# A four-layer graph kernel on one core: layer normalisation's last step on GpSimd, the loops of the graph selected later, and new orders of the jobs

## The chip, the cores and the metric

The kernel runs on one core of a Trainium2 chip. A core has a matrix engine (TensorE, called PE in the profile, with the loading of its weights as PEld), a vector engine (VectorE, DVE), a scalar engine (ScalarE, ACT), GpSimd (POOL) and SyncE (SP), which here only issues DMAs. Each engine works through a queue of its own in order. The metric is the device time of one execution in microseconds (us); lower is better.

## The reference

Input are x, 32 batches of 512 nodes with 64 features, and one graph adj of 512 x 512, symmetric in its pattern, sparse, with a full diagonal. Four layers follow one another, each as "normalise, clip at zero, graph operation, add":

```python
    # --- layer 0 (adj_preln) ---
    h = jnp.maximum(_layernorm(x, axis=-1), 0.0)
    x = x + _L0_gnn_ref(h, adj, ...)
    # --- layer 1 (adj_preln) ---
    h = jnp.maximum(_layernorm(x, axis=-1), 0.0)
    x = x + _L1_gnn_ref(h, 0, L1_gnn_net_params, adj)
    # --- layer 2 (adj_preln) ---
    h = jnp.maximum(_layernorm(x, axis=-1), 0.0)
    x = x + _L2_gnn_ref(h, adj, ...)
    # --- layer 3 (adj_preln) ---
    h = jnp.maximum(_layernorm(x, axis=-1), 0.0)
    x = x + _L3_gnn_ref(h, adj, ...)
```

Layer 0 is three steps of `W2 relu(W1 [v, adj v] + b1) + b2`; before them node 0 of v is set to a given row (`causal_vars.at[:, 0].set(intervention_value)`). Layer 1 is two steps of `relu((adj z) W)`. Layer 2 is attention with eight heads and an output head: scores `h h^T * graph`, zeros of the graph masked, softmax, a weighted sum. Layer 3 is attention with scores made of two vectors, on the graph with its diagonal set to 1 (`adj.at[diag].set(1.0)`). The normalisation is `(x - mean) / sqrt(var + 1e-5)` over the 64 features.

## The kernel before

**Tiling.** Batches go in 16 pairs; a pair's tile has 128 partitions (nodes) and 4 x 2 x 64 columns (node blocks, batches, features). On PE most matmuls use parts of the array: 64 x 64 quarters for scores, 32 x 64 strips for weighted sums, 128 rows for products with the graph. All is fp32, except the mask that is added to the scores.

**Jobs and their order.** The program consists of small named jobs, and three written lists say in which order they are emitted: HEAD (start, with all of pair 0 and much of pair 1), ROUND (once per pair in the middle; `name:lag` means the job of the pair that many rounds back), and TAIL (the last pairs). The lists set the order of each engine's queue; no scheduler changes it. The jobs that are spoken of below, for a pair p:

- `F0` to `F32`: the front, a generator cut at its yields: the layer norm of x (`F0` to `F2`), layer 0 (`F3` to `F20`; `F20` makes x1, L579), the norm of x1 (`F21` to `F23`), layer 1 (`F24` to `F29`; L485 is the product with the graph, L599 makes x2) and the norm of x2 (`F30` to `F32`). `zT` and `zE` turn the result for layer 2 (L473, L478) and copy its halves to the other partitions by DMA (ZZ). `ZQ..` spread z for the weighted sums by DMA.
- Layer 2 has eight units a, b, c, d (first batch) and g, h, i, j (second batch), and f for the output head. For a unit: `s` scores (PE, L641 and L644), `r` row maxima times the graph (DVE, L650), `m` their negation (POOL, L663), `x` exponentials (ACT, L670), `nA`/`nB` the reciprocal (DVE, L680) and the normalising (POOL, L682), `t` block transposes (DVE, L688). For two units: `k`/`Y` the products before the scores (L1139, L1150), `vA` to `vD` the weighted sum (PE, L697), `us`, `w`, `y`, `o`, `c` what follows it, `c` being the sum over heads (cat, L770 and L772).
- Layer 3 is unit e; `oA` to `oC` its norm, `vAE` to `vDE` the weighted sum of f and of the previous pair's e (L925). The last pair does these by batch (O0, O1, L0, L1).
- One-time jobs, in HEAD: `weights`, `joined`, `biases`, `bjoined`, `grams`, `vectors` (weights), `graph0` to `graph3` (the graph turned, L344), `masks` (L367), `factor0` to `factor3` (in place on A2, a copy of the graph, DVE, L371) and `loops0` to `loops3`, which set the diagonal of another copy, A3, to 1: four selects on POOL each (L376). A3 is the last of the three copies of the graph that SP loads (L290, L310, L317) and is used by layer 3 alone.

**The layer norm.** `ln_relu` runs 65 times: four per pair (three in the front, one in `oA` to `oC`), the last pair's fourth in two halves. It has three stages: mean on DVE (L419, L421), centring and squares on POOL (L423, L425); the variance on DVE (L428, L430) and the power -1/2 on POOL (r, L432); last z = max(xc, 0) * r on DVE (L435). In the first of a pair L541 then writes node 0's row into z on DVE and L542 adds a bias to x on POOL.

**The order in HEAD.** loops1, loops0 and loops3 stand between `0.F9` and `0.F12`, in POOL's queue after pair 1's first stage (`1.F0`) and ahead of its second (`1.F1`). In DVE's queue `1.F2` (z of pair 1) and then factor3 stand ahead of `0.F20` (x1 of pair 0).

Of the kernel before, what the change touches and what calls it, by code (L numbers as in the profile page):

```python
# [21 lines left out]
def gnn_stack_kernel(  # L22
# [40 lines left out]
        0.weights 0.F0 0.joined 0.F1 0.F2 0.F3 0.F4 0.biases 0.F5 0.F6 0.graph2 0.graph3 0.graph1 0.graph0 1.F0 0.F7  # L63
        0.F8 0.bjoined 0.F9 0.loops1 0.loops0 0.F10 0.F11 0.masks 0.loops3 0.F12 1.F1 0.factor1 0.F13 0.F14
        0.factor2 0.F15 0.F16 0.F17 1.F2 0.factor3 0.F18 0.grams 0.F19 0.F20 1.F3 2.F0 0.F21 0.F22 0.F23 0.F24 0.F25
        0.F26 1.F4 0.F27 1.F5 0.factor0 0.F28 0.F29 1.F6 0.F30 1.F7 0.F31 1.F8 0.vectors 0.F32 2.F1 0.zT 0.zE 0.k0
        0.Y0 1.F9 0.s0a 1.F10 0.s1a 0.r1a 0.ZQ11 0.r0a 0.r2a 0.m0a 0.x0a 0.s3a 0.r3a 0.s2a 0.m1a 0.r7a 0.r6a 0.r4a
        0.ZQ13 0.x1a 0.s1b 0.m3a 0.r5a 0.s0b 0.k1 0.x3a 0.m2a 0.x2a 0.nAa 0.r3b 0.r2b 0.r1b 0.r0b 0.m1b 0.Y1 0.s3b
        0.nBa 0.t0a 0.r6b 0.s2b 0.r4b 0.r7b 0.x1b 0.m0b 0.ZQ01 0.t1a 0.x0b 0.ZQ03 0.r5b 0.s0c 0.s1c 0.m2b 0.m3b
        0.t2a 1.F11 0.x2b 0.nAb 0.r1c 0.r2c 0.x3b 0.r0c 0.r3c 0.nBb 0.t3a 1.F12 0.t0b 0.m1c 0.t1b 0.m0c 0.x1c 0.s3c  # L70
        1.F13 0.ZQ02 1.F14 0.t3b 0.ZQ00 0.ZQ10 0.x0c 0.t2b 0.r7c 0.r6c 0.s2c 0.vA0 0.vB0 0.r4c 2.F2 0.r5c 0.m3c
        0.s0d 0.m2c 0.vC0 0.vD0 0.r1d 0.nAc 0.r0d 0.s1d 0.m0d 0.x3c 0.t0c 0.x2c 0.us0 0.s2d 0.t1c 0.w00 0.x0d 0.w10
        0.nBc 0.r3d 0.y00 0.r2d 0.t2c 0.m1d 0.t3c 0.ZQ12 0.r5d 0.s3d 0.r7d 0.k2 0.loops2 0.r6d 0.y10 0.o0 0.x1d
        0.r4d 0.m3d 0.Y2 0.x3d 0.m2d 0.nAd 0.c0 0.x2d 0.s1g 1.F15 1.F16 0.r2g 0.s0g 0.t0d 0.nBd 0.t1d 0.r3g 0.t2d
        1.F17 0.t3d 0.s3g 1.F18 0.r7g 0.vA1 0.r6g 0.vB1 1.F19 0.r0g 0.r1g 0.m1g 0.vC1 3.F0 1.F20 0.m3g 0.x1g 0.vD1
        0.m0g 0.s0h 0.s1h 0.r0h 0.r1h 0.us1 0.w01 0.s2g 0.x0g 0.r3h 0.r2h 0.x3g 0.s2h 0.y01 0.k3 0.nAg 0.m0h 0.r4g
        0.r5g 1.F21 0.r4h 0.r5h 0.Y3 0.m2g 0.t0g 0.x2g 0.s3h 0.w11 0.r6h 0.m2h 0.m1h 0.s2i 0.y11 0.nBg 0.x1h 0.x2h
        0.t1g 1.F22 0.r4i 0.s0i 0.t2g 1.F23 1.F24 0.r7h 0.m3h 0.r5i 0.x3h 0.x0h 3.F1 0.s1i 0.r0i 0.nBh 1.F25 0.r1i
        0.o1 0.r3i 0.t3g 0.r2i 0.nAh 1.F26 0.t2h 0.t3h 0.m0i 1.F27 0.t0h 0.t1h 0.s3i 1.F28 0.s1j 0.c1 1.F29 0.m1i
        1.F30 0.x1i 0.vA2 0.r6i 0.m2i 0.vB2 0.x2i 0.x0i 0.vC2 0.r7i 0.vD2 0.s2j 0.r2j 0.m3i 1.F31 0.x3i 0.nAi 0.r3j  # L80
        0.us2 1.F32 1.zT 0.m1j 2.F3 0.nBi 0.s0j 1.zE 0.r5j 0.r4j 2.F4 0.w12 0.t0i 0.x1j 2.F5 0.t2i 0.s3j 1.ZQ00 2.F6
        0.r1j 0.r7j 1.k0 0.y12 0.r0j 0.r6j 0.w02 0.m2j 0.m0j 1.Y0 0.x2j 1.s0a 1.s1a 2.F7 0.t1i 1.r1a 0.m3j 0.t3i
        0.x0j 0.x3j 0.y02 0.nAj 1.r3a 1.r0a 0.D0 1.r2a 2.F8 1.ZQ01 0.t0j 1.m1a 0.o2 1.k1 1.s3a 0.nBj 1.x1a 0.f0
        1.s2a 0.t1j 0.t2j 1.Y1 0.c2 1.m0a 0.t3j 0.vA3 0.vB3 1.ZQ02 1.r4a 1.x0a 1.r5a 1.nAa 0.vC3 0.vD3 1.m2a 1.r7a
        0.us3 1.t1a 1.x2a 3.F2 1.r6a 1.m3a 1.t0a 1.s1b 1.s0b 1.r2b 1.x3a 1.r3b 1.m1b 1.x1b 2.F9 1.ZQ10 1.r1b 1.ZQ12
        1.r0b 1.m0b 2.F10 1.x0b 1.s3b 1.ZQ11 1.s2b 1.nBa 1.r7b 1.r4b 1.r6b 1.m3b 0.w13 1.r5b 1.t2a 0.y13 0.w03 1.x3b
        1.m2b 1.s1c 1.nAb 1.t3a 1.x2b 1.r3c 1.t0b 1.s0c 1.nBb 1.r2c 0.y03 1.r0c 2.F11 2.F12 1.t1b 1.t2b 1.m1c 1.ZQ03
        1.r1c 0.o3 1.s3c 1.t3b 2.F13 1.s2c 1.m0c 0.c3 2.F14 1.r5c 1.x0c 1.vA0 0.D1 1.x1c 1.r6c 1.r4c 1.nAc 1.vB0
        0.f1 1.vC0 1.t0c 1.r7c 1.m2c 1.t1c 1.vD0 0.hQ0 1.x2c 1.s0d 1.us0 1.r1d 1.r0d 1.s1d 1.r3d 1.m3c 1.r2d 1.w00
        1.s2d 1.x3c 1.m0d 1.y00 0.hQ1 1.m1d 1.nBc 1.r4d 1.r5d 1.s3d 1.m2d 1.r6d 1.r7d 1.w10 1.m3d 1.t2c 1.x1d 1.x0d  # L90
        1.nAd 1.y10 1.x3d 1.x2d 0.s3f 1.t3c 1.t0d 0.s1f 1.k2 0.r3f 2.F15 0.hQ2 1.Y2 2.F16 1.nBd 0.r2f 1.o0 1.t1d
        1.t2d 2.F17 0.s0f 1.ZQ13 1.t3d 1.c0 2.F18 0.r7f 1.vA1 0.r1f 1.s0g 0.r6f 0.r0f 0.s2f 2.F19 1.vB1 0.m3f 1.r0g
        1.vC1 0.m0f 2.F20 0.r4f 1.r1g 1.m0g 0.r5f 0.x0f 0.m2f 4.F0 1.vD1 1.s1g 0.x3f 1.us1 0.m1f 1.s3g 2.F21 0.x2f
        1.r3g 1.r2g 1.w01 0.x1f 1.r6g 1.s0h 1.w11 1.m1g 1.r7g 0.nBf 1.r0h 1.s1h 1.x1g 1.r1h 1.s2g 1.y11 0.t2f 0.t3f
        0.nAf 1.x0g 2.F22 1.m0h 1.r5g 1.r2h 1.y01 1.o1 1.m3g 1.r4g 1.r3h 1.m2g 2.F23 0.hQ3 0.t0f 1.x3g 2.F24 1.nAg
        1.x2g 2.F25 0.t1f 1.c1 1.s2h 1.s3h 1.x0h 1.m1h 1.r4h 1.r5h 1.m2h 1.r7h 1.nBg 1.x2h 0.vAE 1.t0g 0.vBE 1.x1h
        0.vCE 0.vDE 0.eu 1.r6h 1.k3 1.t1g 0.et 1.nAh 1.t2g 1.Y3 1.m3h 1.t0h 1.s1i 0.er 1.s0i 1.t3g 1.r2i 2.F26 1.r1i
        1.x3h 1.r3i 1.nBh 2.F27 1.s3i 1.t1h 2.F28 1.r0i 1.t2h 1.t3h 2.F29 1.m1i 2.F30 1.s2i 1.r6i 1.m0i 1.x1i 1.vA2
        1.vB2 1.x0i 1.r7i 1.m3i 1.vC2 1.r4i 1.r5i 2.F31 1.vD2 1.x3i 0.oA 2.F32 1.m2i 1.nAi 1.s1j 1.us2 2.zT 0.oB
        1.r2j 2.zE 1.r3j 1.s0j 1.f0 1.r1j 1.r0j 1.x2i 1.w12 1.y12 1.s3j 3.F3 3.F4 1.m0j 1.s2j 2.ZQ01 2.k0 1.t0i  # L100
        1.r6j 1.w02 1.r7j 1.r5j 1.x0j 1.r4j 2.Y0 2.s0a 2.s1a 1.m3j 1.m1j 2.ZQ02 1.m2j 1.y02 3.F5 1.x1j 1.nBi 3.F6
        1.o2 1.t1i 1.x3j 2.r0a 1.t2i 1.x2j 1.nAj 2.r1a 3.F7 2.r3a 1.t0j 1.D0 1.c2 1.nBj 1.t3i 2.k1 2.r2a 2.m0a 1.t1j
        1.t3j 2.s2a 1.t2j 2.s3a 3.F8 2.m1a 2.Y1 2.r4a 2.x0a 2.r5a 1.vA3 2.r7a 2.x1a 1.vB3 2.nAa 1.vC3 2.m2a 4.F1
        2.t1a 2.x2a 1.vD3 2.t0a 2.r6a 2.s1b 2.s0b 2.m3a 1.us3 0.oC 2.r3b 2.r2b 2.x3a 2.r0b 1.w03 2.m1b 3.F9
    """
    ROUND = """
        r1b:0 s3b:0 y03:1 m0b:0 nBa:0 ZQ00:0 F10:-1 s2b:0 r7b:0 r6b:0 r4b:0 x1b:0 r5b:0 w13:1 ZQ11:0 hQ0:1 x0b:0
        y13:1 t2a:0 s0c:0 m2b:0 m3b:0 x3b:0 nAb:0 s1c:0 t3a:0 x2b:0 r1c:0 F11:-1 t0b:0 r0c:0 nBb:0 r3c:0 t1b:0 r2c:0
        F12:-1 t2b:0 ZQ03:0 o3:1 c3:1 s3c:0 F13:-1 m1c:0 t3b:0 oT:2 s2c:0 m0c:0 F14:-1 r4c:0 f1:1 x1c:0 oE:2 vA0:0
        r7c:0 x0c:0 vB0:0 r5c:0 vC0:0 vD0:0 r6c:0 m3c:0 D1:1 x3c:0 m2c:0 x2c:0 us0:0 nAc:0 t0c:0 nBc:0 t1c:0 s1d:0  # L110
        t2c:0 r2d:0 oN:2 s0d:0 w00:0 r3d:0 oV:2 r1d:0 s2d:0 r0d:0 s3d:0 m1d:0 r4d:0 x1d:0 m0d:0 w10:0 r5d:0 y00:0
        x0d:0 r7d:0 m2d:0 oD:2 oF:2 r6d:0 s1f:1 m3d:0 x2d:0 x3d:0 nAd:0 F15:-1 de:2 r3f:1 t3c:0 t0d:0 nBd:0 r2f:1
        y10:0 k2:0 t1d:0 t2d:0 F16:-1 t3d:0 o0:0 Y2:0 s6e:2 ZQ10:0 F17:-1 hQ1:1 c0:0 F18:-1 s0e:2 vA1:0 r0e:2 F19:-1
        s3e:2 s7e:2 r7e:2 s1e:2 vB1:0 r3e:2 s2e:2 r6e:2 lQ2:2 s0f:1 r2e:2 m3e:2 r1e:2 m1e:2 s5e:2 m0e:2 s4e:2 x0e:2
        m1f:1 F20:-1 r0f:1 x1e:2 hQ2:1 r5e:2 r1f:1 x3e:2 vC1:0 r4e:2 m2e:2 s3f:1 x2e:2 F21:-1 s2f:1 x1f:1 nAe:2
        vD1:0 m0f:1 us1:0 r7f:1 r6f:1 r4f:1 t0e:2 nBe:2 s0g:0 r5f:1 t1e:2 r1g:0 hQ3:1 m3f:1 s1g:0 x0f:1 w01:0 r2g:0
        r0g:0 w11:0 m2f:1 x3f:1 y01:0 nAf:1 x2f:1 m0g:0 r3g:0 t3e:2 t0f:1 y11:0 s3g:0 t2e:2 nBf:1 lQ1:2 x0g:0 lQ0:2
        s2g:0 r7g:0 r6g:0 F22:-1 m1g:0 F23:-1 o1:0 r4g:0 r5g:0 lQ3:2 t1f:1 m3g:0 s1h:0 m2g:0 t2f:1 c1:0 F24:-1 t3f:1
        x1g:0 F25:-1 ZQ12:0 s0h:0 x3g:0 nAg:0 r0h:0 r3h:0 r2h:0 x2g:0 vAE:1 r1h:0 m0h:0 m1h:0 vBE:1 vCE:1 x1h:0
        x0h:0 vDE:1 nBg:0 F0:-3 eu:1 t1g:0 t2g:0 s2h:0 t0g:0 s3h:0 nAh:0 t3g:0 r5h:0 r4h:0 t0h:0 r6h:0 k3:0 Y3:0  # L120
        r7h:0 m2h:0 et:1 s1i:0 s0i:0 m3h:0 ZQ13:0 x2h:0 er:1 F26:-1 x3h:0 r3i:0 r0i:0 nBh:0 r1i:0 t1h:0 t2h:0 r2i:0
        F27:-1 s3i:0 F28:-1 s2i:0 t3h:0 F29:-1 m0i:0 vA2:0 vB2:0 x0i:0 vC2:0 m1i:0 x1i:0 F30:-1 r4i:0 r7i:0 r6i:0
        F2:-2 m3i:0 F31:-1 nAi:0 r5i:0 m2i:0 vD2:0 x3i:0 s2j:0 F32:-1 t0i:0 us2:0 zT:-1 s1j:0 zE:-1 F3:-2 r5j:0 oA:1
        w12:0 x2i:0 F4:-2 r3j:0 r4j:0 r2j:0 y12:0 m2j:0 s0j:0 m1j:0 x1j:0 s3j:0 t1i:0 k0:-1 nBi:0 w02:0 r6j:0 r0j:0
        Y0:-1 r1j:0 r7j:0 t3i:0 s1a:-1 m3j:0 F5:-2 s0a:-1 r2a:-1 t2i:0 y02:0 m0j:0 r0a:-1 F6:-2 x0j:0 nAj:0 x3j:0
# [1220 lines left out]
```

## Time and profile before

| what | us |
|---|---|
| time, median of 3 runs | 2105.23 (2103.9 to 2106.77) |
| the profiled execution: its time | 2107.21 |
| its span, first to last instruction | 2105.4 |
| ACT exponentials L670, 1280 of them, 716 ns each | 909.3 |
| POOL normalising L682, 1280, 704 ns each | 873.6 |
| DVE maxima L650, 1264, 678 ns each | 808.1 |
| DVE transposes L688, 640, 1229 ns each | 776.4 |
| POOL centring L423 / squares L425, about 1.05 us each | 67 / 66 |
| POOL power L432, 128 x 8 values, 1.65 us each | 106.3 |
| DVE last step L435, 63 of 128 x 512, 821 ns each | 51.7 |

A busy time is the union of an engine's instructions; the difference to the span is idle time. The page also has the span in 40 slices, here of 52.6 us, with the busy share in tenths, and the granted clock of PE: it is full in all the middle and lower only in the first two slices and the last. A line of a timeline gives start, duration, engine, source line, operation, what is written and read, the count of merged instructions, and in brackets the idle time of the engine before it and what ended that. In a table of stretches each engine has its busy time and, in brackets, its number of instructions.

### The profile page before, as it was taken

What the parts mean: (1) busy time and instruction counts of PE and PEld (TensorE: products, weight loads), DVE (VectorE), ACT (ScalarE), POOL (GpSimd) and SP (SyncE); (2) the same over time, 40 slices, a digit from 0 to 9 for tenths busy, and PEclk for the clock granted to TensorE, in tenths of its full rate; (3) what the DMA queues carried; (4) which work ended last, traced back from release to release, by engine and by line L of the source; (5) the groups of instructions that cost most, each with busy time, mean ns of one, the idle gap of its engine ahead of it and who ended that gap; (6) DMA issues with size and microseconds to landing.
All of it is one profiled execution on the core that took longest, in us unless ns stands there. A gap on an engine that the chain in (4) does not pass through costs nothing.

```text
span 2105.4 us, 91065 instructions
## 1 busy us (share of the span) xinstructions
PE 2023.7 (96%) x38941; PEld 1218.5 (58%) x38941; DVE 1842.8 (88%) x4205; ACT 1468.8 (70%) x3796; POOL 1274.8 (61%) x2161
## 2 busy tenths in 40 slices
PE   5799999999999999999999999999999999999985
PEld 3356566565556656555665655666565565655554
DVE  3588888989999999999999999999999998899955
ACT  1366667778686777867677786767778677677845
POOL 2356565766666576666657666665766656566543
PEclk9899999999999999999999999999999999999997
DMA  6101101112121111212111111111111111111213
GB/s 135 25 9 27 28 20 34 31 27 43 28 42 26 34 30 27 41 30 42 26 33 27 31 38 33 38 30 32 27 33 38 31 36 35 41 26 33 41 32 74
DMA packets 257626, 74.46 MB, mean 35 GB/s; under 512 B 240324, under 2 KB 249668, under 8 KB 257220
## 3 DMA queue, kind: packets, MB, share of 16 engines
q1 hardware_dynamic: 256768, 68.54, 15.6%
q8 instruction: 305, 5.00, 1.0%
q14 instruction: 101, 0.83, 0.1%
q10 hardware_dynamic: 452, 0.10, 0.0%
HBM read 16.52 MB, written 4.78 MB: 10 GB/s over the span
## 4 chain that ended last, share of the span: by engine, by line
PE 79%; DVE 11%; ACT 3%; POOL 2%; issue 2%; DMA 2%; SPq 0%; ACTq 0%; DVEq 0%; POOLq 0%
PE s L641 21%; PE mm L697 18%; PE mm L758 5%; PE mm L925 5%; PE mm L508 5%; PE s L644 5%; PE mm L738 5%; PE mm L485 4%; DVE sm L688 4%; DVE sm L650 4%; PE mm L1139 3%; PE mm L511 3%; ACT sm L670 2%; POOL sm L682 1%; PE mm L533 1%
## 5 line engine op out<-in xcount | busy, mean ns | idle before, releaser
L670 ACT ACTIVATE sm<-sm,nmx 128x512 f32<-128x512 f32 x1280 | 909.3, 716 | 221.7 <-POOL nmx L663 217.6
L682 POOL TENSOR_SCALAR sm<-sm,rs 128x512 f32<-128x512 f32 x1280 | 873.6, 704 | 275.7 <-DVE rs L680 263.9
L650 DVE CUSTOM_DVE_ANT_0 sm<-s,A 128x512 f32<-128x512 f32 x1264 | 808.1, 678 | 43.5 <-PE s L644 41.2
L688 DVE STREAM_TRANSPOSE sm<-sm 128x1024 f32<-128x1024 f32 x640 | 776.4, 1229 | 78.7 <-POOL sm L682 77.0
L641 PE MATMUL s<-ZZ,Y 64*64 64x512 f32 x4096 | 568.8, 600 | 5.9 <-DVE mx L650 5.7
L697 PE MATMUL mm<-sm,vq 32*64 32x256 f32 (+1 forms) x16640 | 492.9, 376 | 3.9 <-DVE sm L688 3.1
L697 PEld LDWEIGHTS mm<-sm,vq 32*64 32x64 f32 x16640 | 399.3, 132 | 106.9 <-issue 53.8
L663 POOL TENSOR_SCALAR nmx<-mx 128x2 f32<-128x2 f32 x640 | 141.4, 233 | 304.3 <-DVE mx L650 236.3
L641 PEld LDWEIGHTS s<-ZZ,Y 64*64 64x64 f32 x4096 | 143.1, 133 | 185.2 <-DVE mx L650 67.4
L644 PE MATMUL s<-NEGM,I2b 64*64 64x512 bf16 x2288 | 249.3, 376 | 0.0
L670 ACT ACTIVATION_READ_ACCUMULATOR sm<-sm,nmx 128x1 f32 x1280 | 246.3, 192 | 0.0
L644 PEld LDWEIGHTS <-I2b 64*64 64x64 bf16 x2288 | 81.2, 107 | 151.2 <-issue 148.9
L750 ACT ACTIVATE y<-mm,cols 128x512 f32<-128x512 f32 x256 | 161.1, 686 | 9.1 <-PE mm L738 7.6
L738 PE MATMUL mm<-us,Wh 64*64 64x512 f32 x1024 | 141.5, 590 | 1.3 <-ACT hT L478 0.8
L432 POOL TENSOR_TENSOR r<-ve,mhalf 128x8 f32<-128x8 f32 (+1 forms) x65 | 106.3, 1636 | 59.6 <-DVE ve L430 50.8
L423 POOL TENSOR_TENSOR xc<-x,nmu 128x512 f32<-128x512 f32 (+1 forms) x49 | 50.3, 1026 | 142.2 <-DVE nmu L421 135.6
L732 ACT COPY us<-mm 128x256 f32<-128x256 f32 x256 | 76.1, 380 | 85.1 <-PE mm L697 85.1
L485 PE MATMUL mm<-AT,z 128*128 128x512 f32 x256 | 121.4, 618 | 7.1 <-DVE z L435 6.3
L758 PE MATMUL mm<-y,Wo_sb 128*64 128x256 f32 x1024 | 124.1, 384 | 2.1 <-ACT y L750 2.1
L508 PE MATMUL mm<-AT,v 128*64 128x256 f32 x1024 | 117.6, 382 | 0.1
L925 PE MATMUL mm<-sm,vq 32*64 32x256 f32 x3712 | 111.4, 376 | 0.6 <-issue 0.6
L925 PEld LDWEIGHTS mm<-sm,vq 32*64 32x64 f32 x3712 | 101.1, 132 | 13.7 <-DVE rs L680 7.1
(151 smaller groups left out, 1875.6 us busy)
## 6 DMA issues: line engine op xcount, KB each, us to landing
vq<-z SPq DMA_DIRECT2D x512, 32.0 KB
HH<-cat SPq DMA_DIRECT2D x128, 64.0 KB
vq<-catT SPq DMA_DIRECT2D x240, 32.0 KB
vq<-h3n SPq DMA_DIRECT2D x240, 32.0 KB
A<-in_adj_dram SPq DMA_DIRECT2D x5, 1024.0 KB
xt<-in_x_dram SPq DMA_DIRECT2D x32, 128.0 KB
ZZ<-ZZ SPq DMA_DIRECT2D x32, 128.0 KB
out_dram<-xo SPq DMA_DIRECT2D x32, 128.0 KB
```

The costliest lines, as they stand in the source:

```text
L485: nc.tensor.matmul(pe, lhsT=v[:, m].rearrange("p j d -> p (j d)"), rhs=AT[:, m, :], start=(m == 0), stop=(m == NT - 1),)
L508: nc.tensor.matmul(ph[out_, :], lhsT=v[:, m, j, :], rhs=AT[:, m, h], start=False, stop=stop)
L641: nc.tensor.matmul(pss[half][R[ab], :], lhsT=lhsT, rhs=rhs, start=True, stop=False)
L644: nc.tensor.matmul(pss[half][R[ab], :], lhsT=I2b[R[half], :], rhs=NEGM[R[half], k, :], start=False, stop=True)
L650: nc.vector.tensor_tensor_reduce(self.sm[:, s, :], self.pss.pop(s), self.graph(s), 1.0, -FMAX, ALU.mult, ALU.max, self.small("mx", slice(s ...
L670: nc.scalar.activation(self.sm[:, s, :], self.sm[:, s, :], AF.Exp, bias=self.small("nmx", slice(s, s + 1)), accum_out=self.small("ssum", s ...
L682: nc.gpsimd.tensor_scalar(self.sm[:, s, :], self.sm[:, s, :], self.small("rs", slice(s, s + 1)), 1.0, ALU.mult, ALU.mult)
L688: nc.vector.transpose(out=two, in_=two)
L697: nc.tensor.matmul(self.u[i][R[c], 0 : weights.shape[1] * 32], lhsT=values[32 * i : 32 * i + 32, jb, :], rhs=weights[32 * i : 32 * i + 32, ...
L738: nc.tensor.matmul(self.py[ab][c][r, :], lhsT=Wh2[R[c], self.head(c, ab), r], rhs=self.us[R[c], 2 * ab : 2 * ab + 2].rearrange("p i (s e) ...
L758: nc.tensor.matmul(self.pa[R[half], 0 : N // 2], lhsT=Wo_sb[:, self.head(k, ab), :], rhs=self.y[self.head(k, ab)][:, half * N // 2 : (half ...
L925: nc.tensor.matmul(self.u[i][r, 0 : N // 2], lhsT=values[q, jb, :], rhs=unit.sm[q, :, 32 * jb : 32 * jb + 32], start=(jb == 0), stop=(jb = ...
```

## The change

1. The last step of `ln_relu` is two POOL instructions in place of one on DVE: z = xc * r, then z = max(z, 0) * 1, in place.
2. In HEAD the loops are selected later: loops3 after `0.F24`, loops1 and loops2 before `0.F29`, loops0 among the first unit's jobs.
3. All three lists have a new order. HEAD has 761 entries (before 748), ROUND 388 as before, TAIL 1453 (before 1263): TAIL now starts at pair 13's `F22`, with jobs of pairs 10 to 15 in it, where before it started at pair 13's unit b. In HEAD, among others, `0.F1` stands before `joined`, three of the four graph jobs before `0.F5`, `1.F1` and `1.F2` right behind pair 0's start, and `grams` and `vectors` later. The jobs themselves are the same otherwise.

```diff
     HEAD = """
-        0.weights 0.F0 0.joined 0.F1 0.F2 0.F3 0.F4 0.biases 0.F5 0.F6 0.graph2 0.graph3 0.graph1 0.graph0 1.F0 0.F7
-        0.F8 0.bjoined 0.F9 0.loops1 0.loops0 0.F10 0.F11 0.masks 0.loops3 0.F12 1.F1 0.factor1 0.F13 0.F14
-        0.factor2 0.F15 0.F16 0.F17 1.F2 0.factor3 0.F18 0.grams 0.F19 0.F20 1.F3 2.F0 0.F21 0.F22 0.F23 0.F24 0.F25
-        0.F26 1.F4 0.F27 1.F5 0.factor0 0.F28 0.F29 1.F6 0.F30 1.F7 0.F31 1.F8 0.vectors 0.F32 2.F1 0.zT 0.zE 0.k0
-        0.Y0 1.F9 0.s0a 1.F10 0.s1a 0.r1a 0.ZQ11 0.r0a 0.r2a 0.m0a 0.x0a 0.s3a 0.r3a 0.s2a 0.m1a 0.r7a 0.r6a 0.r4a
...
+        0.weights 0.F0 0.F1 0.joined 0.F2 0.F3 0.F4 0.graph3 0.graph1 0.graph2 0.F5 1.F0 0.F6 1.F1 0.graph0 0.biases
+        0.F7 0.F8 0.bjoined 0.F9 0.F10 0.F11 0.F12 1.F2 0.F13 0.F14 0.factor1 0.F15 0.F16 0.F17 0.masks 0.F18 0.F19
+        0.F20 0.F21 1.F3 0.F22 0.F23 0.F24 0.loops3 0.F25 2.F0 0.factor2 0.F26 1.F4 0.F27 1.F5 0.F28 1.F6 0.loops1
+        0.loops2 0.F29 1.F7 0.F30 0.F31 0.factor0 1.F8 0.factor3 0.grams 0.F32 1.F9 0.zT 1.F10 0.vectors 0.zE 0.ZQ13
+        0.k0 2.F1 0.k1 0.Y0 0.s1a 0.r2a 0.r3a 0.s0a 0.ZQ10 0.r0a 0.m1a 0.r1a 0.s3a 0.Y1 0.ZQ00 0.r7a 0.m0a 0.loops0
...
         z = bp.tile([P, NS, D], F32, tag="b", name="z")[:, :g]
-        nc.vector.scalar_tensor_tensor(
-            z, xc, 0.0, r.unsqueeze(2).to_broadcast([P, g, D]), ALU.max, ALU.mult
-        )
+        nc.gpsimd.tensor_tensor(z, xc, r.unsqueeze(2).to_broadcast([P, g, D]), ALU.mult)
+        nc.gpsimd.tensor_scalar(z, z, 0.0, 1.0, ALU.max, ALU.mult)
         return z
```

## The prediction

> **What bounds the kernel now.** I read three views in this order: the page's busy shares and slices, the busy time in stretches of ten us over the head, and then the timeline of the stretch that stood out there; after it the same for one round of the middle. First the page:
>
> ```profile
> PE 2023.7 (96%) x38941; PEld 1218.5 (58%) x38941; DVE 1842.8 (88%) x4205; ACT 1468.8 (70%) x3796; POOL 1274.8 (61%) x2161
> ...
> PE   5799999999999999999999999999999999999985
> ```
>
> TensorE is busy 96% and its holes lie in the first two slices and the last two. In the middle, 150 to 1750 us, it is busy 1595.7 of 1600 us at a granted clock of 1.00. So a change is worth there only what it takes from small stalls; what counts is the head and the end. The head in stretches of ten us (columns: length, then PE, PEld, DVE, ACT, POOL busy, PE clock, DMA share, GB/s):
>
> ```profile
> 30.00:40.00 10.00, 9.54 (x126) 6.48 (x125) 4.47 (x7) 1.81 (x4) 0.00 (x0) 1.00 0.98 210
> 40.00:50.00 10.00, 1.19 (x33) 1.01 (x32) 2.74 (x3) 1.17 (x2) 5.45 (x14) 0.71 0.17 27
> 50.00:60.00 10.00, 2.92 (x34) 2.06 (x35) 6.63 (x11) 0.00 (x0) 6.10 (x5) 0.50 0.00 1
> ```
>
> From 40 to 60 us no compute engine is near full, and POOL does nothing at all from 30 to 40 while the DMA is full. The timeline of that stretch says why:
>
> ```profile
> 42.57 3.01 POOL L376 TENSOR_SCALAR_AFFINE_SELECT A<-A 128x64 f32<-128x64 f32 x12 [16.52 <-DMA A<-in_adj_dram]
> 45.54 1.65 POOL L432 TENSOR_TENSOR r<-ve,mhalf 128x8 f32<-128x8 f32 x1
> ...
> 47.23 1.75 DVE L435 SCALAR_TENSOR_TENSOR z<-xc,r 128x512 f32<-128x512 f32 x1 [11.26 <-POOL r L432]
> ...
> 49.15 1.21 DVE L371 SCALAR_TENSOR_TENSOR A<-A 128x1024 f32<-128x1024 f32 x1
> 50.28 0.73 DVE L579 TENSOR_TENSOR x<-xt,mm 128x256 f32<-128x256 f32 x2
> ...
> 58.53 3.75 PE L485 MATMUL mm<-AT,z 128*128 128x512 f32 x4 [6.35 <-DVE z L435]
> ```
>
> The twelve selects of loops1, loops0 and loops3 (L376) stand in POOL's queue ahead of the power r of pair 1 and wait 16.5 us for A3, the last copy of the graph. Pair 1's z (L435) waits for r in DVE's queue, and behind it stands x1 of **pair 0** (L579), whose matmuls had ended at 39.4. So a wait that concerns layer 3 delays pair 0 by 10.9 us. The chain of waits runs through it: the A DMA to 42.44, the selects, r, z, x1.
>
> In the middle one round is 123.1 us. I looked for the place where PE is late in it:
>
> ```profile
> 1157.78 1.06 PE L641 MATMUL s<-ZZ,Y 64*64 64x512 f32 x4
> 1159.17 0.65 PE L641 MATMUL s<-ZZ,Y 64*64 64x512 f32 x2 [0.33 <-DVE mx L650]
> ```
> ```profile
> 1149.17 1.05 DVE L435 SCALAR_TENSOR_TENSOR z<-xc,r 128x512 f32<-128x512 f32 x1
> 1150.25 1.18 DVE L541 COPY z<-ivt 1x128 f32<-1x128 f32 x1
> ...
> 1154.00 0.69 DVE L435 SCALAR_TENSOR_TENSOR z<-xc,r 128x512 f32<-128x512 f32 x1 [1.11 <-POOL r L432]
> 1155.88 1.25 DVE L688 STREAM_TRANSPOSE sm<-sm 128x1024 f32<-128x1024 f32 x1 [1.19 <-POOL sm L682]
> ```
>
> From 1157.78 to 1163.23 PE does two score jobs (1.07 each elsewhere), one k job (0.92) and one w job (0.86): 3.9 us of work in 5.45, so 1.5 us are lost, because DVE is late with the maxima. Just before, DVE spent 1.05 and 0.69 on two z and 1.11 waiting for r.
>
> **The z on Pool.** Removed: 65 DVE instructions L435, 63 of 128x512 with a mean of 0.821 us and two of 128x256, together 52.6 us, and DVE's 27.7 us of waiting for r. Added: on POOL a two-input multiply like L423 (xc, 1.043) and a one-input, two-operation instruction like L682 (0.704), together 1.75, for 65 about 113 us, so POOL goes from 1275 to 1388 us, 66% of the span. Bounds for one z: 1.7 (rows pipelined) to 2.1. The Trainium skill, GPSIMD Engine Reference, section 4.1, speaks against this: elementwise work belongs on VectorE, and a two-input operation is about twice as slow on GpSimd, a one-input one near line rate. By the rule an estimate is 2 x 0.69 + 0.69 = 2.1 per z, 135 us; the rows here say 1.04 and 0.70, and I take the rows, 2.1 as the upper end. What the rule leaves out is which engine has room: DVE does 114 us of each 123 us round, POOL 79.6.
>
> A second rule is on the change's side: SBUF — State Buffer, "Who interferes with whom", says that a Vector instruction with two SBUF inputs contends with a GpSimd one that reads SBUF. The trace agrees: L435 takes 0.69 alone and 1.05 to 1.75 beside POOL's L542; over 63 that is (0.821 - 0.69) x 63 = 8 us that go with it.
>
> On the **middle**: DVE loses 4 x 0.82 = 3.3 us a round and the waits for r; PE can win back at most the 1.5 us. The order of the whole round is new, so I cannot place the new stall; between 0 and 1.5 I take half, 0.7, for 12 rounds: **-8.4 us** (0 to -18). If POOL's queue makes it worse, see the rival. Changes of PE tile shape cost 0.11 us each (a score job is followed by L697 after 0.31 us instead of 0.20); counted over both orders there are 9 fewer in 440: -1 us, left in the bound.
>
> **The head, step by step.** (1) Pair 0's v, ve and r now come before the joined-weight copies on DVE. sq ends at 7.34, v and ve need 0.9, r 1.66, z 1.75, the L541 copy 0.2: the first transposes (L473) start at 12.3, not 16.55. The graph's data are not late: 1.4 MB had landed by 8 us. Three of the four graph turns now precede F5 on PE and one follows, 3.67 us in all as before; hence L508 starts at about 19.3, before 23.92: -4.6. (2) From L508 to the end of W2T's matmuls the chain is the same, 15.4 us: end at 34.7, before 39.3. The DVE work now ahead of x1 is one factor (waits for A2, landed 29.2, 1.2) and the mask (1.2), done by 33. (3) Nothing of pair 1 holds x1: its z is on POOL by 26, since no select stands ahead. x1 at 34.7, before 50.28. (4) From x1 to L485 before: 8.25 us. Now z needs 1.75 + 0.1 instead of 1.5: 8.5, start at 43.2, before 58.53: **-15.4**. (5) The selects of loops3 follow z on POOL, at 43.0; A3 landed at 42.44, so nothing waits; the eight of loops1 and loops2 take 2 us of the 16 before POOL is next on the chain. (6) L485 to x2's end, 14.7 us, stays. The clock had fallen to 0.50 and four L485 took 6.7 us, at full clock 3.7; PE's hole is now 35.5 to 43.2, 7.7 us, so I leave the slow stretch in; were it gone, 3 us more. (7) x2 to the last transposes before: 7.1, with z at 0.69 after 0.5 of waiting for the copies of vectors ahead of it; now z takes 1.1 more and vectors stands behind, under the 2.2 us ZZ DMA: -14.8. grams' 2.5 us run on PE while POOL does the norm. The ZQ loads are issued behind ZZ's on SP, so they do not hold it. k1 (0.9) now stands ahead of the first score, where 0.6 of pair 1's L523 stood: +0.3. The first score starts at about 72.3, before 86.8: **-14.5**.
>
> From there all work is as before and PE is the bound from 120 on, so the start shifts everything, if the ramp can use it.
>
> **The end.** The tail's order keeps its shape: after pair 15's last cat (before at 2037) PE has about the same 32 us of score, weigh and projection work in both lists, DVE 26 and 27.5. DVE loses 3.3 us per pair where 1750 to 2000 has it busy 229 of 250 and PE only 241; but z of the last two half norms costs 0.61 + 0.38 instead of 0.42 on a chain of latencies. I take **-1 us** (-8 to +4).
>
> Sum: -14.5 - 8.4 - 1 = -23.9. The profiled execution took 2107.2 (span 2105.4); that gives 2083.3. The median of the runs shown is 2.0 below the profiled one: 2081.3, rounded to **2082**.
>
> **Rivals.** (a) *The ramp eats the head.* From 90 to 110 us DVE is busy 9.8 and 9.9 of 10: a unit needs eight maxima (0.61) and four transposes (1.16), 9.6 us, against 4.3 us of scores on PE, until there are weighted sums to do. If pair 1's fronts are used up earlier, PE idles there instead. Against it: the same front jobs of pair 1 lie in the same places. If half of 14.5 is lost and the middle gives nothing: 2105.2 - 7.3 - 1 = 2097.
>
> (b) *POOL's queue becomes the wait: slower.* Place: the point of the round at 1153.96, where four normalising instructions stand behind r and the transpose waits 1.19 for them. With z behind r they start 1.85 later. Price: 4 x 1.85 = 7.4 us a round against some 4 us freed on DVE, so +3.4 x 12 = +41, less 14.5: 2132. It decides once DVE's wait for sm (77 us now) grows by more than 4 us a round. For it: ACT already waits 218 us for nmx from POOL. Against: POOL has 43 us free a round.
>
> (c) *The middle gives back the head:* +1.2 a round, for the same reasons but milder: 2105.
>
> (d) *The selects still wait,* if A3 lands later than 43: they then hold only the next pair's xc; the time is the forecast's within 1 us.
>
> **Chances.** Forecast, with (d): 0.70 (own range 2070 to 2092); (a) 0.14; (c) 0.06; (b) 0.10. The range 2070 to 2100 leaves out (b), (c) and the far side of (a). A measurement here tells about 0.2%, 4 us. Faster: 0.70 and most of (a), 0.82; same: the rest of (a) and (c), 0.08; slower 0.10.
>
> **What would show it.** Right: POOL not idle from 26 to 42 for A3; L579 near 35, the first L485 near 43, the first L641 near 72; L450's two instructions at 1.04 and 0.70; the round at 122 to 123 us; L688's wait for sm no more than about 100 us. Wrong: PE holes between 75 and 130 (a), rounds above 123.5 us with DVE waiting for sm (b).

## The result, and the profile after

| | median of runs, us | range of runs |
|---|---|---|
| before | 2105.27 | 2103.9 to 2106.77 |
| after | 2138.13 | 2136.93 to 2141.37 |
| after / before | 1.0158 | 95% interval 1.0141 to 1.0176 |

The changed kernel is 33 us slower; 2082 was predicted, with 2100 as the upper end. In the changed file the lines of the layer norm stand 14 lower and those behind it 13 lower: L641 is now L654, L485 is L498, L473 is L486, L579 is L592, L682 is L695, L688 is L701, L650 is L663, L925 is L938. The two new instructions are L449 (the multiply) and L450 (the clip).

The page of the changed kernel: the busy line, then TensorE's slices, then the chain that ended last, by engine:

```profile
PE 2016.2 (94%) x38941; PEld 1191.3 (56%) x38941; DVE 1813.1 (85%) x4140; ACT 1464.4 (69%) x3796; POOL 1441.3 (68%) x2291
...
PE   5899999999999999999999999999999999999995
...
PE 53%; POOL 17%; DVE 15%; ACT 7%; issue 4%; SPq 2%; DMA 1%; POOLq 0%; ACTq 0%; DVEq 0%
```

The last of these lines was, in the kernel before:

```profile
PE 79%; DVE 11%; ACT 3%; POOL 2%; issue 2%; DMA 2%; SPq 0%; ACTq 0%; DVEq 0%; POOLq 0%
```

POOL has 166 us more than before, where 113 were added in the prediction. The hole of the second slice is smaller, and no slice of the middle shows a hole, since a loss of 3% is still a "9". The chain shows it: of the path that ended last PE had 79% before and POOL 2%; now PE has 53% and POOL 17%. The groups by line, one row for each shape (busy us, mean ns of one, then idle time before it and what ended it), show which instruction it is:

```profile
L450 POOL TENSOR_SCALAR z<-z 128x512 f32<-128x512 f32 x63 | 123.3, 1957 | 5.7
...
L449 POOL TENSOR_TENSOR z<-xc,r 128x512 f32<-128x512 f32 x63 | 65.7, 1043 | 1.2
...
L486 PE MATMUL mm<-ident,z 64*64 64x64 f32 x1504 | 33.7, 230 | 36.5 <-POOL z L450 32.7 <-DVE z L554 3.7
```

The multiply takes what was predicted, 1.04. The clip takes 1.96 instead of 0.70. One z is 3.0 us instead of 1.75, and TensorE's transposes of z (L486) stand 32.7 us waiting for it. The view of waits has this from both of PE's queues, and also what did not grow (us in total, times, longest):

```profile
DVE sm L663 <- PE s L657: 86.0, 90, 4.6
...
DVE sm L701 <- POOL sm L695: 71.4, 90, 2.0
...
PEld mm L486 <- POOL z L450: 44.4, 18, 3.5
...
PE mm L498 <- POOL z L450: 13.6, 13, 10.3
DVE z L554 <- POOL z L450: 13.1, 13, 2.0
```

The same two waits of DVE in the kernel before:

```profile
DVE sm L688 <- POOL sm L682: 77.0, 104, 2.3
...
DVE sm L650 <- PE s L644: 41.2, 83, 2.7
```

DVE's wait for the normalising (L701, before L688) was 77.0 us and is 71.4: POOL's queue does not hold the softmax up more than before. DVE's wait for scores (L663, before L650) was 41.2 and is 86.0: it is PE that is late. (Not all of that rise costs time: in e1 below, which is fast, it is 67.1.) One such place, in the timeline of a round in the middle:

```profile
1042.44 1.04 POOL L449 TENSOR_TENSOR z<-xc,r 128x512 f32<-128x512 f32 x1
...
1043.57 1.95 POOL L450 TENSOR_SCALAR z<-z 128x512 f32<-128x512 f32 x1
...
1045.58 0.69 PE L486 MATMUL mm<-ident,z 64*64 64x64 f32 x32 [2.60 <-POOL z L450]
...
1046.09 1.04 PE L654 MATMUL s<-ZZ,Y 64*64 64x512 f32 x8
...
1047.37 0.69 DVE L663 CUSTOM_DVE_ANT_0 sm<-s,A 128x512 f32<-128x512 f32 x1 [2.65 <-PE s L657]
```

PE comes to the transposes in its queue 2.6 us before z is there. Scores of another pair stand behind them, need nothing from z, and wait too; then the maxima on DVE wait for these scores. In five of the rounds the granted clock also falls to 0.50 for a few us around a hole of PE; behind the one that ends at 539.56, for instance, a group of eight scores takes 1.93 us in place of the 1.04 above. Rounds, measured from one pair's first L938 (L925) to the next, were 123.1 to 123.6 us over most of the middle and are 125.9 to 128.0. From 150 to 1750 us PE is busy 1550.9 us, before 1595.7.

The head got shorter, though by less than predicted (columns: length, PE, PEld, DVE, ACT, POOL busy, PE clock, DMA share, GB/s; then its timeline):

```profile
40.00:50.00 10.00, 2.01 (x3) 0.98 (x4) 3.29 (x5) 0.00 (x0) 8.54 (x10) 0.55 0.27 42
50.00:60.00 10.00, 8.51 (x88) 3.83 (x90) 0.00 (x0) 2.54 (x7) 2.74 (x9) 0.93 0.01 2
```
```profile
37.30 0.75 DVE L592 TENSOR_TENSOR x<-xt,mm 128x256 f32<-128x256 f32 x2 [2.33 <-PE mm L536]
...
43.96 1.04 POOL L449 TENSOR_TENSOR z<-xc,r 128x512 f32<-128x512 f32 x1
...
45.09 2.85 POOL L450 TENSOR_SCALAR z<-z 128x512 f32<-128x512 f32 x1
47.90 1.03 POOL L390 TENSOR_SCALAR_AFFINE_SELECT A<-A 128x64 f32<-128x64 f32 x4
...
47.99 1.22 PE L498 MATMUL mm<-AT,z 128*128 128x512 f32 x1 [10.28 <-POOL z L450]
```

x1 comes at 37.3, before 50.3; the selects (L390) follow z and wait for nothing; but PE stands 10.3 us before its product with the graph, and the last 2.85 of them are the clip.

The span, cut at four points of each trace, puts the loss in one stretch. "e1" is the experiment below, in which the second instruction of z is fast:

| stretch, us | before | after | e1 |
|---|---|---|---|
| to the first score | 86.8 | 77.8 | 72.8 |
| to the first weighted sum of layer 3 | 180.5 | 179.8 | 176.7 |
| from there 14 rounds | 1716.5 | 1760.5 | 1705.1 |
| rest to the end | 121.6 | 116.8 | 117.1 |
| span | 2105.4 | 2134.9 | 2071.7 |

After gains 9.0 + 0.7 + 4.8 outside the rounds and loses 44.0 in them: +29.5. The profiled execution of e1 was the fastest of its four, 5 us below their median, so its column is a little too good.

### The profile page after: what moved, and what is told of

It reads as the page before. It is cut to its first block, busy times and chain, and to the rows that moved or that the text cites. A ratio compares the mean times of both kernels' runs of the same rounds, so it can differ in the third digit from the quotient of the medians.

```text
span 2134.9 us, 91110 instructions
## 1 busy us (share of the span) xinstructions
PE 2016.2 (94%) x38941; PEld 1191.3 (56%) x38941; DVE 1813.1 (85%) x4140; ACT 1464.4 (69%) x3796; POOL 1441.3 (68%) x2291
## 4 chain that ended last, share of the span: by engine, by line
PE 53%; POOL 17%; DVE 15%; ACT 7%; issue 4%; SPq 2%; DMA 1%; POOLq 0%; ACTq 0%; DVEq 0%
PE s L654 13%; PE mm L710 11%; DVE sm L663 8%; POOL sm L695 7%; ACT sm L683 5%; PE mm L938 5%; PE mm L521 5%; POOL z L450 4%; DVE sm L701 4%; PE mm L771 4%; PE s L657 3%; PE mm L751 3%; PE mm L524 2%; PE mm L1152 2%; POOL z L449 2%
## 5 line engine op out<-in xcount | busy, mean ns | idle before, releaser
L695 POOL TENSOR_SCALAR sm<-sm,rs 128x512 f32<-128x512 f32 x1280 | 862.9, 692 | 216.4 <-DVE rs L693 209.4
L663 DVE CUSTOM_DVE_ANT_0 sm<-s,A 128x512 f32<-128x512 f32 x1264 | 805.7, 679 | 91.1 <-PE s L657 86.0
L701 DVE STREAM_TRANSPOSE sm<-sm 128x1024 f32<-128x1024 f32 x640 | 775.3, 1229 | 74.5 <-POOL sm L695 71.4
L654 PE MATMUL s<-ZZ,Y 64*64 64x512 f32 x4096 | 557.7, 601 | 5.0 <-ACT Y L1163 2.7
L710 PE MATMUL mm<-sm,vq 32*64 32x256 f32 (+1 forms) x16640 | 485.9, 376 | 2.8 <-DVE sm L701 1.1
L710 PEld LDWEIGHTS mm<-sm,vq 32*64 32x64 f32 x16640 | 386.1, 132 | 116.3 <-issue 55.0
L676 POOL TENSOR_SCALAR nmx<-mx 128x2 f32<-128x2 f32 x640 | 134.2, 218 | 291.0 <-DVE mx L663 255.3
L657 PE MATMUL s<-NEGM,I2b 64*64 64x512 bf16 x2288 | 242.6, 377 | 0.0
L654 PEld LDWEIGHTS s<-ZZ,Y 64*64 64x64 f32 x4096 | 139.4, 133 | 167.0 <-issue 61.6
L498 PE MATMUL mm<-AT,z 128*128 128x512 f32 x256 | 121.7, 619 | 18.0 <-POOL z L450 13.6
L751 PE MATMUL mm<-us,Wh 64*64 64x512 f32 x1024 | 132.6, 594 | 0.8 <-ACT us L745 0.8
L450 POOL TENSOR_SCALAR z<-z 128x512 f32<-128x512 f32 (+1 forms) x65 | 125.4, 1930 | 5.9
L521 PE MATMUL mm<-AT,v 128*64 128x256 f32 x1024 | 117.6, 382 | 0.1
L938 PE MATMUL mm<-sm,vq 32*64 32x256 f32 x3712 | 108.9, 376 | 2.5 <-DVE sm L701 2.5
## 6 DMA issues: line engine op xcount, KB each, us to landing
xt<-in_x_dram SPq DMA_DIRECT2D x32, 128.0 KB
ZZ<-ZZ SPq DMA_DIRECT2D x32, 128.0 KB
out_dram<-xo SPq DMA_DIRECT2D x32, 128.0 KB
```

What stands on the lines that cost most here:

```text
L450: nc.gpsimd.tensor_scalar(z, z, 0.0, 1.0, ALU.max, ALU.mult)
L521: nc.tensor.matmul(ph[out_, :], lhsT=v[:, m, j, :], rhs=AT[:, m, h], start=False, stop=stop)
L654: nc.tensor.matmul(pss[half][R[ab], :], lhsT=lhsT, rhs=rhs, start=True, stop=False)
L657: nc.tensor.matmul(pss[half][R[ab], :], lhsT=I2b[R[half], :], rhs=NEGM[R[half], k, :], start=False, stop=True)
L663: nc.vector.tensor_tensor_reduce(self.sm[:, s, :], self.pss.pop(s), self.graph(s), 1.0, -FMAX, ALU.mult, ALU.max, self.small("mx", slice(s ...
L695: nc.gpsimd.tensor_scalar(self.sm[:, s, :], self.sm[:, s, :], self.small("rs", slice(s, s + 1)), 1.0, ALU.mult, ALU.mult)
```

## The experiments

The theory is that the second POOL instruction is of a slow form and that PE, which takes its queue in order, pays for each microsecond of z. Rivals are POOL's queue as a whole (the softmax held up behind z, or POOL simply too full), and the new orders being worse whatever z costs. Ratios are to the kernel before, run on the same chip with each group.

**e2: what POOL's instructions cost by themselves.** At the end of the kernel before, 32 POOL instructions on one 128x512 tile are added, in groups of four.

```diff
+    for n in range(4):
+        nc.gpsimd.tensor_scalar(bx, bx, 0.0, 1.0, ALU.max, ALU.mult)
...
+        nc.gpsimd.tensor_scalar(bx, bx, 1.0, 1.0, ALU.mult, ALU.mult)
...
+        nc.gpsimd.tensor_scalar(bx, bx, 0.0, None, ALU.max)
...
+        nc.gpsimd.tensor_scalar(bx, bx, 1.0, None, ALU.mult)
...
+        nc.gpsimd.tensor_scalar(bx, bx, bz[:, 0, 0:1], 1.0, ALU.max, ALU.mult)
...
+        nc.gpsimd.tensor_scalar(bx, bx, 1.0, 0.0, ALU.mult, ALU.max)
...
+        nc.gpsimd.tensor_scalar(by, bx, 0.0, 1.0, ALU.max, ALU.mult)
...
+        nc.gpsimd.tensor_tensor(by, bx, bz, ALU.mult)
```

> The kernel before, with 32 more POOL instructions on a 128x512 tile behind its last job, in groups of four alike, while DVE is nearly done. Theory M (the form with a maximum is itself slow): max,mult with constants 1.9 us each as in the changed kernel, mult,mult 0.70; which of max alone, mult alone, a pointer scalar, the order mult,max and another output tile is slow is open. Theory C (the 1.94 us of the changed kernel come from what runs beside it, or from working in place behind the multiply): every one-input form 0.70 here. The time itself is some 40 us longer and says nothing.

POOL's timeline at the end of this kernel; each row is four instructions, in the order of the diff, with the short gaps between them:

```profile
2107.28 7.94 POOL L1309 TENSOR_SCALAR xt<-xt 128x512 f32<-128x512 f32 x4 [16.16 <-DMA xt<-in_x_dram]
2115.31 2.72 POOL L1311 TENSOR_SCALAR xt<-xt 128x512 f32<-128x512 f32 x4
2118.11 6.19 POOL L1313 TENSOR_SCALAR xt<-xt 128x512 f32<-128x512 f32 x4
2124.38 6.20 POOL L1315 TENSOR_SCALAR xt<-xt 128x512 f32<-128x512 f32 x4
2130.68 8.26 POOL L1317 TENSOR_SCALAR xt<-xt,bz 128x512 f32<-128x512 f32 x4
2139.03 7.94 POOL L1319 TENSOR_SCALAR xt<-xt 128x512 f32<-128x512 f32 x4
2147.05 7.93 POOL L1321 TENSOR_SCALAR by<-xt 128x512 f32<-128x512 f32 x4
2155.07 5.28 POOL L1323 TENSOR_TENSOR by<-xt,bz 128x512 f32<-128x512 f32 x4
```

One instruction without the gaps (median of the four): the pair (mult, mult) takes 0.62 us; with a pointer for the first operand that is the form of the normalising. Every other one-input form tried takes 1.48 to 1.99: max alone 1.48, even mult alone 1.49, (max, mult) and (mult, max) 1.92, with a pointer for the first operand 1.99; another output tile changes nothing. All other engines had ended by 2103.6. So the 1.96 of L450 is nearly all the instruction's own: with nothing beside it, it takes 1.92.

**e1: the change with a fast second instruction.** This leaves out the clip.

```diff
-        nc.gpsimd.tensor_scalar(z, z, 0.0, 1.0, ALU.max, ALU.mult)
+        nc.gpsimd.tensor_scalar(z, z, 1.0, 1.0, ALU.mult, ALU.mult)
```

> The changed kernel with the second POOL instruction as mult by 1, mult by 1: it leaves out the clip at zero. Theory M: the instruction falls from 1.94 to 0.70 us, the waits of PE for z go from 77 to under 20 us, the round from 126.3 to about 123, and the time to 2085 to 2100. Theory Q (two more instructions of any length in POOL's queue delay the normalising and so the transposes): the round stays above 125 and the time at 2120 or more.

2078.86 us, ratio 0.9874 (0.9857 to 0.9891). It is faster than either range that was expected. Nothing but 1.34 us per z is different from the changed kernel, and 59 us of time are gone. Its head:

```profile
34.56 0.75 DVE L592 TENSOR_TENSOR x<-xt,mm 128x256 f32<-128x256 f32 x2 [2.33 <-PE mm L536]
...
42.34 0.62 POOL L450 TENSOR_SCALAR z<-z 128x512 f32<-128x512 f32 x1
...
43.01 5.49 PE L498 MATMUL mm<-AT,z 128*128 128x512 f32 x6 [8.03 <-POOL z L450]
```

and its wait of the transposes' weight loads for z, 44.4 in the changed kernel:

```profile
PEld mm L486 <- POOL z L450: 9.1, 13, 2.2
```

The matmuls of L486 themselves wait 2.1 us for it, 32.7 in the changed kernel. From the second to the tenth, rounds are 121.6 to 122.5 us. POOL still does 1352 us of work, 77 more than before, and all orders are the new ones. So neither the added load of POOL as such nor the orders made the change slow.

**e11: a dose between.** The second instruction is given twice in the fast form, so that one z takes 1.05 + 2 x 0.62, with the gaps some 2.4 us. This too leaves out the clip.

```diff
-        nc.gpsimd.tensor_scalar(z, z, 0.0, 1.0, ALU.max, ALU.mult)
+        nc.gpsimd.tensor_scalar(z, z, 1.0, 1.0, ALU.mult, ALU.mult)
+        nc.gpsimd.tensor_scalar(z, z, 1.0, 1.0, ALU.mult, ALU.mult)
```

> The changed kernel with the slow second POOL instruction replaced by two of the fast form (mult by 1, mult by 1, 0.62 each); it leaves out the clip. z then takes 1.04 + 0.62 + 0.62 + gaps, some 2.4 us, between the 1.7 of the run with one of them (2078.9) and the 3.0 of the changed kernel (2138.1). Theory L (what counts is only how late z comes for PE, and the orders leave no slack for more than 1.7): in proportion, 2105 to 2115. Theory F (the slow form does harm besides its length, for instance to DVE): nearer to the run with one, 2080 to 2095.

2104.93 us, 0.9995 (0.9985 to 1.0004): as fast as before, to the tenth of a per cent, and at the low end of theory L's range; theory F is out. Work of POOL for one z, without gaps, against time: 1.66 gives 2078.9, 2.28 gives 2104.9, 3.00 gives 2138.1. That is +26 and +33 us, or over 63 z 0.41 us for each 0.62 and 0.53 for each 0.72: some 0.7 us of time for each microsecond of z, over the range of 1.66 to 3.00 us. PEld's wait for z goes along, 9.1, 27.1, 44.4 us. Below 1.66 the price is lower: e10 further down, with a z of 1.04 us on POOL, is 11 us faster than e1, about 0.3 for each microsecond, though its clip also stands in DVE's queue.

**e3: the new orders alone**, with z on DVE in one instruction as before.

```diff
-        nc.gpsimd.tensor_tensor(z, xc, r.unsqueeze(2).to_broadcast([P, g, D]), ALU.mult)
-        nc.gpsimd.tensor_scalar(z, z, 0.0, 1.0, ALU.max, ALU.mult)
+        nc.vector.scalar_tensor_tensor(
+            z, xc, 0.0, r.unsqueeze(2).to_broadcast([P, g, D]), ALU.max, ALU.mult
+        )
```

> The three new orders with z on DVE as before, one instruction. Theory M or Q (POOL is at fault): the head's 9 us and more stay, the round is 123 to 124: 2088 to 2100. Theory O (the new orders of ROUND and TAIL are worse by themselves): the round stays above 125: 2120 to 2140.

2088.72 us, 0.9924 (0.9909 to 0.9939), first score at 69.7. That is as theory M or Q expected. The orders are worth 16 us without the move to POOL, all of it in the head: the 14 rounds together take 1717.4 us, before 1716.5. On top of them z on POOL brings another 10 us in the fast form (e1) and costs 49 in the slow one.

**e5 and e7: which part of the orders.** e5 is the kernel before with only the loops moved; e7 is the kernel before with the whole new HEAD and the old ROUND and TAIL. z is on DVE in both.

```diff
-        0.F9 0.loops1 0.loops0 0.F10 0.F11 0.masks 0.loops3 0.F12
+        0.F9 0.F10 0.F11 0.masks 0.F12
...
-        0.F24 0.F25
+        0.F24 0.loops3 0.F25
...
-        0.F28 0.F29
+        0.F28 0.loops1 0.F29
...
-        0.m1b 0.Y1 0.s3b
+        0.m1b 0.Y1 0.loops0 0.s3b
```

(This is the diff of e5, by jobs; e7's is the HEAD part of the diff of the change.)

> The kernel before with the loops alone moved in HEAD: loops3 after F24 of pair 0, loops1 after F28, loops0 after Y1. By the prediction's head step x1 of pair 0 starts near 39.5 instead of 50.3 and the rest follows: 2093 to 2097. Rival a (the ramp, where DVE is full, eats the head's gain): 2100 or more.

> The new HEAD alone; ROUND, TAIL and z on DVE as before. By the orders-only run (2088.7, first score at 69.7 us against 86.8, rounds 122.5 against 123.1 to 123.4) the head is worth up to 17 and twelve rounds some 8. If the head's gain is kept whole: 2088 to 2091, and then the new ROUND gives nothing in sum because the new TAIL takes it back. If the ramp takes a part: 2092 to 2098.

e5 takes 2096.4 us, 0.996 (0.995 to 0.997), first score at 75.8; x1 of pair 0 starts at 39.5 as expected, so the selects did hold it; e7 takes 2090.37, 0.993 (0.9915 to 0.9945), first score at 70.8. So the late selects carry 9 of the 15 us that the new head brings, and the head carries nearly all of what the orders bring. In both the first score moves by a little more than the time does (11.0 for 9, 16.0 for 15), which is hardly more than the runs' scatter; what is lost is lost behind it.

**e4: z on POOL alone**, in the two instructions of the change, with the old orders.

```diff
-        nc.vector.scalar_tensor_tensor(
-            z, xc, 0.0, r.unsqueeze(2).to_broadcast([P, g, D]), ALU.max, ALU.mult
-        )
+        nc.gpsimd.tensor_tensor(z, xc, r.unsqueeze(2).to_broadcast([P, g, D]), ALU.mult)
+        nc.gpsimd.tensor_scalar(z, z, 0.0, 1.0, ALU.max, ALU.mult)
```

> Part 1 of the change alone: the orders of before, z in two POOL instructions with the clip (3.0 us). Theory L: z comes 2.1 us later than by DVE, four times a round; where PE stands waiting in both orders alike the loss is as in the changed kernel against the orders alone, +49 us: 2140 to 2165, with no gain in the head. If the orders of before have more slack behind z: 2110 to 2135.

2273.45 us, 1.0801 (1.0785 to 1.0817), over 100 us above either range; most rounds take 133 to 135 us. Its timeline at one z (here L432 is r, L681 the normalising, L435 and L436 are z):

```profile
1109.79 1.67 POOL L432 TENSOR_TENSOR r<-ve,mhalf 128x8 f32<-128x8 f32 x1 [0.77 <-DVE rs L679]
...
1111.45 2.70 POOL L681 TENSOR_SCALAR sm<-sm,rs 128x512 f32<-128x512 f32 x4
...
1115.44 1.94 POOL L436 TENSOR_SCALAR z<-z 128x512 f32<-128x512 f32 x1
...
1117.43 1.14 PE L472 MATMUL mm<-ident,z 64*64 64x64 f32 x32 [7.60 <-POOL z L436]
1118.34 1.94 PE L640 MATMUL s<-ZZ,Y 64*64 64x512 f32 x8
```

In the old order four normalising instructions stand between r and z. z on DVE did not have to wait for them; on POOL z stands behind them, and PE waits 7.6 us. The hole costs more than itself: the granted clock is 0.50 from 1114 to 1122, and eight scores take 1.94 us in place of 1.09 just before the hole. This comes back in nearly every round, and over the run PE is busy 2065.9 us with the same number of matmuls for which it needed 2023.7 before. The new orders are no ornament of the change: without them the move costs 167 us.

**e9 and e10: the clip back on DVE, in two places.** Both keep the new orders and one POOL multiply. e9 clips z behind the multiply; e10 clips xc, which is there before r is, right behind the issue of r. Since r is positive, max(xc, 0) * r is what the reference has.

```diff
 e9
         nc.gpsimd.tensor_tensor(z, xc, r.unsqueeze(2).to_broadcast([P, g, D]), ALU.mult)
-        nc.gpsimd.tensor_scalar(z, z, 0.0, 1.0, ALU.max, ALU.mult)
+        nc.vector.tensor_scalar(z, z, 0.0, None, ALU.max)
 e10
         nc.gpsimd.tensor_tensor(r, ve, mhalf[:, :g], ALU.pow)
+        nc.vector.tensor_scalar(xc, xc, 0.0, None, ALU.max)
         yield
...
         nc.gpsimd.tensor_tensor(z, xc, r.unsqueeze(2).to_broadcast([P, g, D]), ALU.mult)
-        nc.gpsimd.tensor_scalar(z, z, 0.0, 1.0, ALU.max, ALU.mult)
```

> The changed kernel with the clip on DVE behind POOL's multiply, not ahead of it: z comes after 1.04, a wait between the engines and 0.4 on DVE, and it also stands in DVE's queue. Theory L: z comes later than with the early clip (2067.7) and about as with mult,mult (2078.9), if DVE is free just then: 2072 to 2085. If DVE's queue holds it up: 2085 to 2110.

> The changed kernel with the clip done on DVE, on xc, while POOL computes the power r; z is then one POOL multiply of 1.04. The result is the same. Theory L: z comes 0.6 us earlier than in the run with mult,mult (2078.9), DVE has 65 clips of 0.4 to 0.7 more: 2072 to 2084, the shortest of all so far. If DVE's clip meets POOL's instructions[...], or DVE is the bound: 2084 to 2095.

e10 takes **2067.72 us, 0.9819 (0.9803 to 0.9836)**: 38 us faster than the kernel before and 70 faster than the changed one, with most rounds at about 121 us, and 4 us below theory L's range. e9 takes 2150.41, 1.0208 (1.0193 to 1.0223), slower than either kernel and 40 us above both ranges, though POOL does the same work to 5 us and DVE's 65 clips last 29 us against 27. The waits and the timeline of e9 say why:

```profile
DVE z L450 <- POOL z L449: 101.4, 36, 5.0
```
```profile
1043.65 0.43 DVE L450 TENSOR_SCALAR z<-z 128x512 f32<-128x512 f32 x1 [2.89 <-POOL z L449]
1044.00 0.68 DVE L663 CUSTOM_DVE_ANT_0 sm<-s,A 128x512 f32<-128x512 f32 x1
```

The clip stands in DVE's queue right where z was on DVE, but now it waits there for a product that POOL makes after r; the maxima of the softmax stand behind it. That is 2.8 us at each of 36 places. In e10 the same instruction waits 0.3 us in all.

**e12: the early clip with the old orders** (e10's layer norm in the kernel before).

> All three orders of before, with z as one POOL multiply of 1.04 and the clip on DVE while r is computed. It tells how much of the 2273.5 of the old orders with z on POOL is the slow form (1.9 us of 3.0) and how much is the place of z in POOL's queue, behind the four normalising instructions. If the form is all of it: z comes about as soon as with DVE, 2100 to 2115. If the place is most of it: 2160 to 2250.

2172.96 us, 1.0307 (1.0286 to 1.0328), most rounds 127 to 128.5. The time lies in the range for "the place is most of it", but that name does not fit: of the 167 us of e4 the short z saves 100, and 67 remain. Against e10, whose z is the same, the old orders cost 105 us. Here too the clock falls in most rounds, and PE is busy 2046.5 us.

## Why the prediction was wrong

**The step that failed** is the term "a one-input, two-operation instruction like L682 (0.704)" in "The z on Pool". It measured 1.96, so one z was 3.0 us and lay outside the bounds of 1.7 to 2.1. The rest of the mechanism held; this term was mis-sized, and no term of the sum gave a price to a z that comes later. I took the price from a row with the same engine, the same tile and the same number of operations, but with the operations mult and mult; the new instruction is max and mult, and e2 shows that this decides. The trace of before has no other one-input POOL instruction on a tile of this size, so the row was the nearest only in shape, and the upper bound of 2.1 was held by the rule of the Trainium skill, GPSIMD Engine Reference, section 4.1, that a one-input operation runs near line rate. The measurement decides: on this tile that holds for (mult, mult) alone, of the forms that were tried. The rule's advice, that elementwise work belongs on VectorE, held: the same clip takes 0.42 us there (e10).

**The rest of the sum** can be read from e1, where z takes 1.66 us and all else is as changed. It is 26.6 us faster than the kernel before, where the sum said 23.9; the parts fit less well than the total, since the middle and the end gave more than their terms. The head went as written:

| step | predicted | e1 | after |
|---|---|---|---|
| (1) first transposes (L486) | 12.3 | 12.38 | 15.47 |
| (1) first product with the graph (L521, before L508) | 19.3 | 19.05 | 21.78 |
| (3) x1 | 34.7 | 34.56 | 37.30 |
| (4) first L498 | 43.2 | 43.01 | 47.99 |
| (7) first score | 72.3 | 72.83 | 77.80 |

The last column falls behind by 3.1 us before the first transposes. Of this 1.0 was there before the clip began, 1.3 is the clip, and 1.1 is a copy of one row on DVE (L554) that takes 1.28 us while POOL's L555 runs and 0.20 in e1, where it does not; e1 also waits 0.3 us on DVE at that place. At the product with the graph 2.2 more are lost to the clip that took 2.85. Step (5), that the selects wait for nothing, was right too; rival (d) did not occur.

**The middle:** -0.7 a round was predicted for a z of 1.75; e1 has rounds of 122.3 against 123.3 in the mean of the eleven from the second to the twelfth, so -1.0. It was left open where the new stall would be; it is at L486. What was not seen is that PE has no slack there: the forecast put no price on z coming later ("between 0 and 1.5 I take half"), and e11 shows 0.7 us lost for each microsecond added. A price for that was what the rivals lacked. Taken from e1 and e11 alone it is 0.67; for the 1.34 us of the slow clip 0.67 x 1.34 x 63 gives +57, and after is 59 above e1. The clock that falls in five rounds of after is in this price.

**The end** was to give -1 and gave -4.8 in after and -4.5 in e1, inside its bounds. In e3, with the same orders and z on DVE, that stretch takes 121.0 us, so the gain did not come from the orders alone; it was not tried apart.

**A reading.** The prediction saw that L435 takes longer beside POOL's two-input instructions, and read the contention off that side alone. Its 0.69 us were often not "alone": in twelve cases L682 ran beside L435 all the time, and it was mostly L682 that became longer. Of the 21 L682 that overlap an L435 by more than 0.3 us, sixteen take 1.11 to 1.23 us, where one without takes 0.70. So more than the 8 us went with L435. No term of the sum rests on it.

**The rivals.** (a), the ramp eating the head: e5 and e7 show 2 and 1 us of it at most, e1 none. (c), the middle giving back the head, is what after shows and more (-9.0 and +44.0), but not for its reasons, which were (b)'s. (b) named a time, 2132, that is near the result of 2138, but that is luck, since its mechanism did not happen: it said that the normalising instructions start later behind z and that DVE's wait for sm grows by more than 4 us a round. That wait shrank from 77.0 to 71.4. In the new ROUND z stands where POOL has room, and it is PE that waits for z itself. With the old order the place of (b) is real, seen the other way round: there z waits for the normalising, and DVE's wait for sm is 125.0 us in e4.

Of the signs that were named for "right", L450's 0.70, the L592 near 35, the L498 near 43 and the round of 122 to 123 failed together, nearly all by the same instruction, and so did the first score near 72; the L701 sign held and so ruled out (b).

## What to carry to other kernels

Price a new instruction by a row with the same engine, shape **and operations**; where the trace has none, the bounds must allow for a form several times slower, or the instruction must be measured alone before anything is built on it. When a step moves to an engine that has time to spare, look at who stands in order behind its result: POOL had 43 us free in each round, and still each microsecond of z beyond 1.66 cost 0.7. And if a step waits for a late value, take out of it the part that does not need that value and do it earlier: the clip of xc in e10, off the chain, made a version that beats both kernels.

## What the runs showed of the hardware

One-input instructions on POOL for 128x512 fp32 take 0.62 us as (mult, mult) with constants (e2) and 0.70 with a pointer for the first operand (the normalising before, 704 ns), but 1.48 or 1.49 with one operation, be it max or mult, and 1.92 as (max, mult) or (mult, max). So a multiplication by 1 and by 1 is 2.4 times as fast as a single multiplication by 1. The runs do not show why; a multiply of two inputs is between them, 1.26 in e2, 1.04 where r is broadcast and 1.05 where one tile is squared (L425 before). PE's granted clock falls to 0.50 around holes: in e4 PE stops at 1109.8, the clock is 1.00 until 1112 and 0.50 from 1114, and it is full again from 1124, some 6 us after PE went on. One clip in the head took 2.85 us (from 45.09) where 63 have a mean of 1.96; DVE's L385, with two inputs in SBUF, ran beside it from 44.94 to 46.15, but whether that lengthened it was not tried.
